# Last map of a two-layer decoder: gate products on two column tiles of the array, LoRA products on four row tiles

## Chip, cores and metric

The kernel runs on one core of a Trainium2 chip. The metric is the device time of one execution in microseconds; "us" is that throughout. Engines are named as in the profile: PE is TensorE (with PEld, its weight loads), DVE is VectorE, ACT is ScalarE, POOL is GpSimd, SP is SyncE, which issues most DMAs.

## What is computed

Two batches of 512 tokens with 1024 features pass through two decoder layers. Each layer is a cross attention and an FFN with LoRA. The change is about the very last part, the FFN of the second layer (called the last map here). Cut to what matters:

```python
x = x + _L1_xattn_ref(_layernorm(x), ctx, ctx, mask, wq, wk, wv, wo, 0)
x = x + _L1_ffn_ref(_layernorm(x), W_up, gate_w, expert_bias, lora_A, lora_B)

def _L1_ffn_ref(x, W_up, gate_w, expert_bias, lora_A, lora_B):   # E = 4 experts, R = 8
    logits = x_flat @ gate_w.T + expert_bias
    one_hot = jax.nn.one_hot(jnp.argmax(logits, axis=-1), 4)
    base_out = jnp.einsum('bth,oh->bto', x, W_up)
    z = jnp.einsum('nh,erh->ner', x_flat, lora_A)
    d = jnp.einsum('ner,ehr->neh', z, lora_B) * SCALE            # SCALE = 1
    return base_out + jnp.einsum('neh,ne->nh', d, one_hot)
```

So for every token there are 4 gate logits and 32 LoRA values (36 columns, one matrix `ga_t`), the best expert is chosen, the 8 values of that expert are kept and the other 24 are set to zero, and the 32 values are multiplied by a 32 x 1024 matrix and added to the 1024 x 1024 map. All matrix products here are in f32.

## The kernel before

**The map.** A 512 x 1024 by 1024 x 1024 product is done with seven block products in place of eight (a Winograd form of Strassen's scheme). `token_sums` makes the seven left operands from normed and transposed rows (L245, L248, L250, L253 on DVE), `right_sums` the seven right operands from four 512 x 512 quarters of the weight (L259, L262, L264, L267 on DVE). `linear` (L572) gives two chains of seven block products, one for each half of the tokens in a block, `blocks(0)` and `blocks(1)`, which `pair` interleaves for the first two products and then runs one after the other. Each block product is four accumulated matmuls of 128x128 by 128x512 on TensorE, issued by `accumulate` at L347. `seven_onto` (L304) takes them in the order 1, 2, 6, 7, 5, 4, 3 and adds them to the rows: product 1 is copied to a tile u by ACT (L315), product 6 is added to u by DVE (L317), each other product is added by DVE straight to its quarter of the rows (L320), and where u belongs too (products 5, 4 and 3), POOL adds it afterwards (L322). The row quarters are called (0,0), (1,1), (1,0) and (0,1).

**LoRA before.** `lora` in `linear` hangs one more matmul on products 2, 4, 5 and 3 of each chain: eight for a map and sixteen for the two batches. It contracts over all 128 partitions, of which 32 hold something; the rest of z and of the LoRA matrix (L1232, one load of 128 x 1024) is zero. The third operand it needs is the difference of the two token halves (`split_tokens`, L596).

**Gates before.** `gated` (L947) is a generator. For each of four groups of 128 tokens, eight matmuls take the tokens as the stationary operand (128x128) and `ga_t` (36 columns) as the moving one (L954), into one tile of type "wide". Then DVE does for each group of tokens seven small operations (L966 to L978): add the bias, take the maximum, compare, prefer the first of equals, compare again, and multiply the 32 values by the choice into a tile z, which POOL has set to zero (L976, two memsets of 128x256). Four transposes on TensorE (L988) and a DVE copy (L989) give z transposed.

**What sets the order.** TensorE's queue follows the order of the program text exactly. In the attention loop that order is written by hand for DVE, ACT and POOL as well: `attention` (L847) yields three times for each head, and `hooks` (L1194 to L1214) attach actions to a head and a phase. The last heads share their time with the beginning of the last map of batch 0: the weights are fetched at hook (61, 2), the gate products stand at (62, 1), the gate arithmetic at (62, 2), and the transposes of z with the first two block products at (63, 1). After L1236 a scheduler orders DVE, ACT, POOL and SP. There `turned_and_gated` (L1248) weaves the norms, transposes (L204) and gates of batch 1 into the map of batch 0.

**The softmax around it.** For each head POOL sums the exponentials (L811, L814, L815, L816), TensorE transposes the sums (L723), DVE reduces them (L725), and a row goes through DRAM (L732, L738); DVE adds the negative maximum to the scores (L805) and ACT takes the exponential (L808). L822 is the product with the values; the projection with wo (`projection`, L835) also goes through `seven_onto` and L347, in blocks of two matmuls.

**Buffers.** PSUM has two "wide" tiles (two banks each) and four "b" tiles (one bank each). The transposes of rows (L202) and of softmax sums (L721) use wide tiles.

Of the kernel before, what the change touches and what calls it, by code (L numbers as in the profile page):

```python
# [15 lines left out]
ALU = mybir.AluOpType  # L16
AX = mybir.AxisListType

P = 128
B, S, D = 2, 512, 1024  # L20
# [4 lines left out]
E1, R1 = 4, 8  # L25
# [6 lines left out]
NT = S // P  # L32
NC = D // P
NKT = S2 // P
HALF = 512
# [4 lines left out]
def decoder_kernel(  # L40
# [25 lines left out]
    nc = tc.nc  # L66
# [39 lines left out]
    ident = const.tile([P, P], F32, name="ident")  # L106
# [194 lines left out]
                emit(0, 1, u)  # L301
            yield

    def seven_onto(product, place, order=(1, 6, 2, 7, 5, 4, 3)):  # L304

        banks = {}
        for i in order:
            first = {2: 1, 4: 7, 3: 5}.get(i, i)
            if i == first:
                banks[i] = ps_b()  # L310
            acc = banks[first]
            product(i, acc, i == first)
            if i == 1:
                u = u2([P, HALF])
                nc.scalar.copy(u, acc)  # L315
            elif i == 6:
                nc.vector.tensor_tensor(u, u, acc, ALU.add)  # L317
            else:
                c = place(*{2: (0, 0), 7: (1, 1), 5: (1, 1), 4: (1, 0), 3: (0, 1)}[i])
                nc.vector.tensor_tensor(c, c, acc, ALU.add)  # L320
                if i != 2 and i != 7:
                    nc.gpsimd.tensor_tensor(c, c, u, ALU.add)  # L322
            yield

    def pair(a, b):
# [15 lines left out]
    def advance(stretches, n):  # L341
        for _ in range(n):
            next(stretches)
# [27 lines left out]
    def rows(b, t):  # L371
        return x[b][t // 2][:, t % 2, :]
# [158 lines left out]
    def normed(b, tile, n, ready=None):  # L531

        if n == 2:
            hs = [tile([P, 4, S]) for _ in range(2)]
            quarters = [[hs[ch][:, :, ts(th, 256)] for ch in range(2)] for th in range(2)]
        else:
            quarters = [[tile([P, 4, 256]) for _ in range(2)] for _ in range(2)]
        steps = transposed_norm(
            b,
            [[quarters[t // 2][j][:, :, ts(t % 2, P)] for t in range(NT)] for j in range(2)],  # L540
            ready,
        )
# [29 lines left out]
    def linear(b, h_ops, w_ops, tT, bl):  # L572

        def blocks(s):
            lora = {2: (0, 0), 4: (1, 0), 5: (1, 1), 3: (2, 1)}

            def product(i, acc, start):
                pairs = [
                    (h_ops[i - 1][:, c, ts(s, P)], w_ops(i, c))
                    for c in range(4)  # L580
                ]
                if i in lora:
                    th, nh = lora[i]
# [3 lines left out]
            return seven_onto(  # L587
                product,
                lambda i, j: rows(b, 2 * i + s)[:, ts(j, HALF)],
                (1, 2, 6, 7, 5, 4, 3),  # L590
            )
# [355 lines left out]
    def gated(quarters):  # L947


        zT, diff = u2([P, S]), u2([P, 256])  # L950
        gaccs = ps_wide().rearrange("p (t n) -> p t n", t=NT)
        for t in range(NT):
            for c in range(NC):
                nc.tensor.matmul(  # L954
                    gaccs[:, t, :NGA],
                    chunk(quarters, c, t),
                    ga_t[:, c, :],
                    start=(c == 0),
                    stop=(c == NC - 1),
                )  # L960
            yield
        zs = []
        for t in range(NT):
            gacc = gaccs[:, t, :]
            lg = small([P, E1])
            nc.vector.tensor_tensor(lg, gacc[:, :E1], eb_t, ALU.add)  # L966
            mx = small([P, 1])
            nc.vector.tensor_reduce(mx, lg, AX.X, ALU.max)

            nc.vector.tensor_scalar(lg, lg, mx, None, ALU.is_equal)  # L970
            nc.vector.tensor_tensor(lg, lg, prefer, ALU.mult)
            nc.vector.tensor_reduce(mx, lg, AX.X, ALU.max)
            nc.vector.tensor_scalar(lg, lg, mx, None, ALU.is_equal)
            if t % 2 == 0:
                z2 = u2([P, 2, P])
                nc.gpsimd.memset(z2, 0.0)  # L976
            z = z2[:, t % 2]
            nc.vector.tensor_tensor(  # L978
                z[:, : E1 * R1].rearrange("p (e r) -> p e r", r=R1),
                gacc[:, E1:NGA].rearrange("p (e r) -> p e r", r=R1),  # L980
                lg.unsqueeze(2).to_broadcast([P, E1, R1]),
                ALU.mult,
            )
            zs.append(z)
        yield
        tr = ps_tr()
        for t, z in enumerate(zs):
            nc.tensor.transpose(tr[:, t, :], z, ident)  # L988
        nc.vector.tensor_copy(zT, tr.rearrange("p t n -> p (t n)"))  # L989
        yield split_tokens(zT, diff)  # L990


    ctx.enter_context(tc.manual_schedule(engines={mybir.EngineType.PE}))
# [117 lines left out]
    bl_t = u8([P, D])  # L1111
# [64 lines left out]
    def turn_row(t):  # L1176
        transposed(
            last["rows"][:, t % 2, :],
            [last["hs"][t // 2][j][:, :, ts(t % 2, P)] for j in range(2)],
        )  # L1180
# [5 lines left out]
            wupT[ts(ch, 4 * P), ts(nh, HALF)].rearrange("(c p) n -> p c n", p=P),  # L1186
        )

    def begin_map():
        hs = last["hs"]  # L1190
        last["h"][:2] = hs[0]
        last["gates"] = gated(hs)

    hooks = {(42, 0): [lambda: next(stats)], (42, 1): [turn_away]}  # L1194
    for t in range(NT):
# [1 line left out]
    for i in range(2):  # L1197
        n = 44 + 4 * i
        hooks[(n, 2)] = [lambda i=i: fetch_half(i)]
        hooks[(n + 1, 1)] = [lambda i=i: scale_row(2 * i)]  # L1200
        hooks[(n + 2, 1)] = [lambda i=i: turn_row(2 * i), lambda i=i: scale_row(2 * i + 1)]
        hooks[(n + 3, 1)] = [lambda i=i: turn_row(2 * i + 1)]
    hooks[(61, 2)] = [
        lambda: fetch_weight(1, 0, 0),
        lambda: fetch_weight(2, 1, 0),
        lambda: fetch_rows(0),
        begin_map,
    ]
    hooks[(62, 1)] = [lambda: advance(last["gates"], 4)]
    hooks[(62, 2)] = [  # L1210
        lambda: next(last["gates"]),
        lambda: fetch_weight(7, 0, 1),
        lambda: fetch_weight(3, 1, 1),
    ]  # L1214
    with tc.manual_schedule(
        engines={
            mybir.EngineType.DVE,
            mybir.EngineType.Activation,
            mybir.EngineType.Pool,
        }  # L1220
    ):
        for i in range(3 * (B * NH + 2)):
            next(steps)
            n, phase = divmod(i, 3)
            for act in hooks.get((n - 2, phase), ()):
                act()
            if (n - 2, phase) == (63, 1):
                zTs = [next(last["gates"]), None]
                h_ops, parts = last["h"], last["w"]
                w_ops = lambda i, c: parts[i - 1][:, c, :]  # L1230
                bl_t = u4([P, D])
                nc.sync.dma_start(bl_t, bl1T)  # L1232
                main = linear(0, h_ops, w_ops, lambda: zTs[0], bl_t)
                advance(main, 2)

    h_ops[:] = token_sums(last["hs"], lambda: u4([P, 4, 256]))  # L1236
# [5 lines left out]
    advance(main, 5)  # L1242
    for _ in steps:
        pass
    hs, norms = normed(1, u4, 4)
    gates = gated(hs)

    def turned_and_gated():  # L1248
        next(norms)
        yield  # L1250
        next(norms)
        yield
        for _ in range(3):
            next(norms)
            next(gates)
            yield
        next(gates)
        yield
        next(gates)
        yield  # L1260
# [16 lines left out]
def rope_tables():  # L1277
# [68 lines left out]
```

## Time and profile before

| what | value |
|---|---|
| median of 3 runs | 2475.18 us (2473.69 to 2479.97) |
| profiled execution | 2474.92 us |
| its span in the trace | 2473.1 us |
| mean granted TensorE clock | 0.993 |
| TensorE idle before L347, all of the kernel | 19.1 us, most of it for the first loads |
| L954, gate products | 128 instructions of 128x36, 2273.4 to 2408 |
| L759, scores | 1024 of 128x512, 454.3 us busy |
| L773, DVE add of 128x1024 from PSUM | mean 1224 ns |
| L320, DVE add of 128x512 from PSUM | mean 680 ns |

Columns of a row are explained where it is shown. A matmul's end is modelled in the trace, so the distance between starts is a better measure of its cost than the length shown. A weight load (LDWEIGHTS) overlaps the matmul before it. A matmul in f32 shows as two pairs of weight load and matmul. The timeline merges neighbours of one kind into one line with a count.

### The profile page before, as it was taken

How to read it: one execution, taken by the hardware profiler on the slowest of the kernel's cores; microseconds unless marked ns; L12 is line 12 of the kernel's file. 1: busy time of each engine (PE TensorE's matmuls, PEld its weight loads, DVE VectorE, ACT ScalarE, POOL GpSimd, SP SyncE). 2: the span in 40 equal slices, each digit the busy share in tenths (PEclk: the TensorE clock that was granted, in tenths of full speed). 3: DMA queues.
4: the chain of work that ended last, by engine and by line, in shares of the span. 5: the costliest groups of instructions: out<-in, count | busy, mean ns of one | idle time of the engine just before them, and what ended most of it. 6: DMA issues, size and time to landing. Idle time of an engine off the chain costs nothing.

```text
span 2473.1 us, 19694 instructions
## 1 busy us (share of the span) xinstructions
PE 2432.6 (98%) x6856; PEld 1218.4 (49%) x6856; DVE 1835.2 (74%) x2020; ACT 528.1 (21%) x615; POOL 1028.8 (42%) x552
## 2 busy tenths in 40 slices
PE   8999999999999999999999999999999999999998
PEld 3477458654444444444444444444444444445453
DVE  4949674346886547898888888888888888886552
ACT  1211221001122222222222222222222222222100
POOL 0000010111000002686767767776767676767421
PEclk9999999999999999999999999999999999999999
DMA  5437142013895221344323432443334333323301
GB/s 181 179 120 255 69 146 97 22 68 111 296 333 187 74 98 41 106 128 115 103 76 90 115 95 81 128 149 89 105 110 129 79 94 108 112 72 103 128 26 43
DMA packets 148819, 288.02 MB, mean 116 GB/s; under 512 B 29360, under 2 KB 47296, under 8 KB 146416
## 3 DMA queue, kind: packets, MB, share of 16 engines
q1 hardware_dynamic: 107888, 244.35, 29.4%
q10 hardware_dynamic: 40400, 41.70, 6.9%
q8 instruction: 55, 0.90, 0.2%
q0 software_dynamic: 432, 0.71, 0.1%
q14 instruction: 44, 0.36, 0.1%
HBM read 223.54 MB, written 63.18 MB: 116 GB/s over the span
## 4 chain that ended last, share of the span: by engine, by line
PE 79%; DVE 8%; POOL 3%; issue 2%; DMA 2%; ACT 1%; SPq 0%; ACTq 0%; POOLq 0%; DVEq 0%
PE b L347 45%; PE wide L759 15%; PE b L822 14%; DVE u L805 2%; PE wide L723 2%; PE wide L460 1%; PE wide L204 1%; POOL u L815 1%; POOL u L814 1%; DVE u L783 1%; DMA u<-in_wo_dram 1%; DVE u L785 1%; PE wide L954 1%; DVE small L725 1%; DMA row<-small 1%
## 5 line engine op out<-in xcount | busy, mean ns | idle before, releaser
L347 PE MATMUL b<-u,u 128*128 128x512 f32 (+1 forms) x3648 | 1407.8, 544 | 19.1 <-DMA u<-in_ctxT_in_dram 7.8
L347 PEld LDWEIGHTS b<-u,u 128*128 128x128 f32 x3648 | 693.6, 191 | 698.7 <-issue 619.2
L822 PE MATMUL b<-u,u 128*128 128x512 f32 x1024 | 462.3, 595 | 0.0
L759 PE MATMUL wide<-u,u 128*128 128x512 f32 x1024 | 454.3, 595 | 7.2 <-DVE u L773 6.3
L773 DVE TENSOR_TENSOR u<-wide,u 128x1024 f32<-128x1024 f32 x256 | 312.9, 1224 | 133.1 <-PE wide L759 132.9
L808 ACT ACTIVATE u<-u 128x2048 f32<-128x2048 f32 x128 | 244.6, 1911 | 653.8 <-DVE u L805 619.9
L759 PEld LDWEIGHTS wide<-u,u 128*128 128x128 f32 x1024 | 193.9, 190 | 256.0 <-issue 176.7
L805 DVE TENSOR_TENSOR u<-u,b 128x2048 f32<-128x2048 f32 x128 | 290.2, 2268 | 0.0
L811 POOL TENSOR_TENSOR u<-u 128x1024 f32<-128x1024 f32 x64 | 151.4, 2366 | 319.8 <-ACT u L808 319.8
L822 PEld LDWEIGHTS b<-u,u 128*128 128x128 f32 x1024 | 187.3, 193 | 185.6 <-issue 185.6
L322 POOL TENSOR_TENSOR u<-u,u 128x512 f32<-128x512 f32 x120 | 188.7, 1592 | 197.5 <-DVE u L320 177.9
L320 DVE TENSOR_TENSOR u<-u,b 128x512 f32<-128x512 f32 x200 | 135.9, 680 | 135.4 <-PE b L347 135.4
L222 POOL TENSOR_TENSOR u<-u,sin_t 128x512 f32<-128x512 f32 x8 | 11.6, 1455 | 387.8 <-ACT u L217 387.8
L814 POOL TENSOR_TENSOR u<-u,u 128x1024 f32<-128x1024 f32 x64 | 150.8, 2356 | 35.6 <-ACT u L808 35.2
L815 POOL TENSOR_TENSOR u<-u,u 128x1024 f32<-128x1024 f32 x64 | 151.6, 2369 | 5.0
L833 POOL TENSOR_TENSOR u<-u,u 128x512 f32<-128x512 f32 x64 | 117.7, 1839 | 21.8 <-DMA u<-row 21.8
L216 ACT ACTIVATE u<-u 64x512 f32<-64x512 f32 x72 | 45.2, 628 | 356.1 <-DVE u L293 177.9
L603 POOL TENSOR_TENSOR u<-u,u 128x1024 f32<-128x1024 f32 x8 | 20.2, 2532 | 231.5 <-DVE u L168 228.9
L723 PEld LDWEIGHTS wide<-ident,u 128*128 128x128 f32 x512 | 80.1, 204 | 64.5 <-issue 54.3
L781 DVE TENSOR_TENSOR u<-u 128x1024 f32<-128x1024 f32 x64 | 110.4, 1725 | 0.0
L783 DVE TENSOR_TENSOR u<-u,u 128x1024 f32<-128x1024 f32 x64 | 106.1, 1658 | 0.2
L816 POOL TENSOR_TENSOR u<-u 128x512 f32<-128x512 f32 x64 | 101.4, 1584 | 5.0
(127 smaller groups left out, 1624.8 us busy)
## 6 DMA issues: line engine op xcount, KB each, us to landing
u<-row ACTq DMA_DIRECT2D x128, 256.0 KB, 3.7
u<-wo SPq DMA_DIRECT2D x64, 512.0 KB, 4.2
u<-in_wo_dram SPq DMA_DIRECT2D x48, 512.0 KB, 4.5
u<-in_wq_dram SPq DMA_DIRECT2D x32, 512.0 KB, 4.2
q<-u SPq DMA_DIRECT2D x64, 256.0 KB, 2.6
u<-in_wo_dram SPq DMA_DIRECT2D x16, 1024.0 KB, 8.1
wo<-u SPq DMA_DIRECT2D x32, 512.0 KB, 4.4
u<-q SPq DMA_DIRECT2D x64, 256.0 KB, 4.2
```

Of the source, the lines that this page charges most:

```text
L320: nc.vector.tensor_tensor(c, c, acc, ALU.add)
L322: nc.gpsimd.tensor_tensor(c, c, u, ALU.add)
L347: nc.tensor.matmul(acc, lhsT, rhs, start=start and k == 0, stop=k == len(pairs) - 1, skip_group_check=True,)
L759: nc.tensor.matmul(sc[:, ts(n, HALF)], self.kT[:, ts(2 * j + n, P)], self.qT, start=True, stop=True,)
L773: nc.vector.tensor_tensor(self.e[j // 2][:, js, :], sc.rearrange("p (k q) -> p k q", k=2), mask[j], ALU.add)
L783: nc.vector.tensor_tensor(m, m, e[1][:, 0:2, :], ALU.max)
L805: nc.vector.tensor_tensor(e, e, self.nmf.unsqueeze(1).to_broadcast([P, 4, S]), ALU.add)
L808: nc.scalar.activation(e, e, AF.Exp)
L811: nc.gpsimd.tensor_tensor(d, e[:, 0:2, :], e[:, 2:4, :], ALU.add)
L814: nc.gpsimd.tensor_tensor(d, d, e[:, 0:2, :], ALU.add)
L815: nc.gpsimd.tensor_tensor(d, d, e[:, 2:4, :], ALU.add)
L822: nc.tensor.matmul(self.acc, self.v[:, k, :], self.e[j][:, k % 4, :], start=(k == 0), stop=(k == NKT - 1),)
```

## The change

Gates: `ga_t` becomes the stationary operand (36 columns) and 256 tokens the moving one, so that 16 matmuls do what 32 did. Even chunks of the contraction go to partitions 0 to 35 of a bank and odd ones to 64 to 99; that places them on the two 64-column tiles of the array. ACT copies both halves to a tile that POOL has set to zero one phase earlier, TensorE transposes that tile (four), and DVE adds the two halves and does the gate arithmetic for all four groups of tokens at once. z is written four times side by side, so that its transpose holds it on partitions 0, 32, 64 and 96.

LoRA: the products leave `linear`, and `split_tokens` is no longer called here. `add_lora` makes two parts of four matmuls, each with 32 rows of contraction on a row tile of its own and into a bank of its own (two wide tiles), and DVE adds them to the rows. The matrix is loaded four times, to 32 partitions each. The parts stand between products of the map.

Rows: with `u_first`, which every `linear` now uses (both FFNs), POOL adds u to the three quarters as soon as product 6 is in, ahead of DVE's adds of products 7, 5, 4 and 3. Row tile 1 of batch 1, the last to be complete, is stored in two halves.

In the queues, the zeros go to hook (61, 1), the gate products and their arithmetic both to (62, 1). On SP the load of weight quarter 7 goes ahead of three wo loads and that of quarter 3 ahead of two.

```diff
-    def seven_onto(product, place, order=(1, 6, 2, 7, 5, 4, 3)):
+    def seven_onto(product, place, order=(1, 6, 2, 7, 5, 4, 3), u_first=False):
...
             elif i == 6:
                 nc.vector.tensor_tensor(u, u, acc, ALU.add)
+                if u_first:
+                    for k in (5, 4, 3):
+                        add(place(*places[k]), u)
             else:
-                c = place(*{2: (0, 0), 7: (1, 1), 5: (1, 1), 4: (1, 0), 3: (0, 1)}[i])
+                c = place(*places[i])
                 nc.vector.tensor_tensor(c, c, acc, ALU.add)
-                if i != 2 and i != 7:
-                    nc.gpsimd.tensor_tensor(c, c, u, ALU.add)
+                if i != 2 and i != 7 and not u_first:
+                    add(c, u)
...
-            lora = {2: (0, 0), 4: (1, 0), 5: (1, 1), 3: (2, 1)}
+            lora = {} if tT is None else {2: (0, 0), 4: (1, 0), 5: (1, 1), 3: (2, 1)}
...
     def gated(quarters):
-        zT, diff = u2([P, S]), u2([P, 256])
-        gaccs = ps_wide().rearrange("p (t n) -> p t n", t=NT)
-        for t in range(NT):
+        sums = u2([P, S])
+        nc.gpsimd.memset(sums, 0.0)
+        yield
+        parts = [slice(64 * i, 64 * i + NGA) for i in range(2)]
+        for th in range(2):
+            acc = ps_b()
             for c in range(NC):
                 nc.tensor.matmul(
-                    gaccs[:, t, :NGA],
-                    chunk(quarters, c, t),
+                    acc[parts[c % 2], 0:256],
                     ga_t[:, c, :],
-                    start=(c == 0),
-                    stop=(c == NC - 1),
+                    quarters[th][c // 4][:, c % 4, :],
+                    start=(c < 2),
+                    stop=(c >= NC - 2),
                 )
-            yield
+            for part in parts:
+                nc.scalar.copy(sums[part, ts(th, 256)], acc[part, 0:256])
+            yield
...
+        for t in range(NT):
+            nc.tensor.transpose(tr[:, t, :], sums[:, ts(t, P)], ident)
+        nc.vector.tensor_copy(both, tr[:, :, parts[0]])
+        nc.vector.tensor_tensor(both, both, tr[:, :, parts[1]], ALU.add)
...
+        for k in range(4):
             nc.vector.tensor_tensor(
-                z[:, : E1 * R1].rearrange("p (e r) -> p e r", r=R1),
...
+                z[:, :, ts(k, E1 * R1)].rearrange("p t (e r) -> p t e r", r=R1),
...
+    def add_lora(b, zT, bl):
+        K = E1 * R1
+        for i in range(2):
+            accs = [ps_wide() for _ in range(2)]
+            for k in range(4):
+                j, nh = k // 2, k % 2
+                nc.tensor.matmul(
+                    accs[j][:, ts(nh, HALF)],
+                    zT[ts(k, K), ts(2 * i + j, P)],
+                    bl[ts(k, K), ts(nh, HALF)],
+                    start=True,
+                    stop=True,
+                )
+            for j in range(2):
+                xs = rows(b, 2 * i + j)
+                nc.vector.tensor_tensor(xs, xs, accs[j], ALU.add)
+            yield
...
+    hooks[(61, 1)] = [begin_gates]
...
-    hooks[(62, 1)] = [lambda: advance(last["gates"], 4)]
+    hooks[(62, 1)] = [lambda: advance(last["gates"], 3)]
     hooks[(62, 2)] = [
-        lambda: next(last["gates"]),
...
-                nc.sync.dma_start(bl_t, bl1T)
-                main = linear(0, h_ops, w_ops, lambda: zTs[0], bl_t)
+                for k in range(4):
+                    nc.sync.dma_start(bl_t[ts(k, E1 * R1), :], bl1T[: E1 * R1, :])
+                main = linear(0, h_ops, w_ops, None, None)
...
     def turned_and_gated():
+        next(lora)
         next(norms)
         yield
...
+        next(gates)
         next(norms)
         yield
-        for _ in range(3):
-            next(norms)
-            next(gates)
-            yield
+        next(norms)
+        yield
         next(gates)
+        next(lora)
         yield
...
-    main = linear(1, token_sums(hs, lambda: u4([P, 4, 256])), w_ops, lambda: zTs[1], bl_t)
+    main = linear(1, token_sums(hs, lambda: u4([P, 4, 256])), w_ops, None, None)
     advance(main, 2)
-    zTs[1] = next(gates)
+    zT = next(gates)
+    lora = add_lora(1, zT, bl_t)
+    for _ in range(2):
+        advance(main, 2)
+        next(lora)
...
-    for t in range(NT):
+    for t in (0, 2, 3):
         nc.sync.dma_start(out[1, ts(t, P), :], rows(1, t))
+    for i in range(2):
+        nc.sync.dma_start(out[1, ts(1, P), ts(i, HALF)], rows(1, 1)[:, ts(i, HALF)])
```

More of the change, by code (lines that the diff above doesn't have):

```diff
@@ L302, in seven, with add @@
             yield
-    def seven_onto(product, place, order=(1, 6, 2, 7, 5, 4, 3)):
+    def seven_onto(product, place, order=(1, 6, 2, 7, 5, 4, 3), u_first=False):
         banks = {}
+        places = {2: (0, 0), 7: (1, 1), 5: (1, 1), 4: (1, 0), 3: (0, 1)}
+        def add(c, what):
+            nc.gpsimd.tensor_tensor(c, c, what, ALU.add)
         for i in order:
@@ L590, in blocks @@
                 (1, 2, 6, 7, 5, 4, 3),
+                True,
             )
@@ L957, in gated @@
                     ga_t[:, c, :],
-                    start=(c == 0),
-                    stop=(c == NC - 1),
-                )
+                    quarters[th][c // 4][:, c % 4, :],
+                    start=(c < 2),
+                    stop=(c >= NC - 2),
+                )
+            for part in parts:
+                nc.scalar.copy(sums[part, ts(th, 256)], acc[part, 0:256])
             yield
-        zs = []
+        zT = u2([P, S])
+        z = u2([P, NT, P])
+        tr, both = ps_tr(), u2([P, NT, NGA])
@@ L963, in gated @@
         for t in range(NT):
[L964 to L977, printed above, removed]
+            nc.tensor.transpose(tr[:, t, :], sums[:, ts(t, P)], ident)
+        nc.vector.tensor_copy(both, tr[:, :, parts[0]])
+        nc.vector.tensor_tensor(both, both, tr[:, :, parts[1]], ALU.add)
+        lg = small([P, NT, E1])
+        by_expert = lambda t: t.unsqueeze(1).to_broadcast([P, NT, E1])
+        nc.vector.tensor_tensor(lg, both[:, :, :E1], by_expert(eb_t), ALU.add)
@@ L978, in gated @@
+        mx = small([P, NT])
+        by_token = mx.unsqueeze(2).to_broadcast([P, NT, E1])
+        nc.vector.tensor_reduce(mx, lg, AX.X, ALU.max)
+        nc.vector.tensor_tensor(lg, lg, by_token, ALU.is_equal)
+        nc.vector.tensor_tensor(lg, lg, by_expert(prefer), ALU.mult)
+        nc.vector.tensor_reduce(mx, lg, AX.X, ALU.max)
+        nc.vector.tensor_tensor(lg, lg, by_token, ALU.is_equal)
+        for k in range(4):
             nc.vector.tensor_tensor(
-                z[:, : E1 * R1].rearrange("p (e r) -> p e r", r=R1),
@@ L980, in gated @@
-                gacc[:, E1:NGA].rearrange("p (e r) -> p e r", r=R1),
-                lg.unsqueeze(2).to_broadcast([P, E1, R1]),
+                z[:, :, ts(k, E1 * R1)].rearrange("p t (e r) -> p t e r", r=R1),
+                both[:, :, E1:].rearrange("p t (e r) -> p t e r", r=R1),
+                lg.unsqueeze(3).to_broadcast([P, NT, E1, R1]),
                 ALU.mult,
             )
-            zs.append(z)
         yield
         tr = ps_tr()
-        for t, z in enumerate(zs):
-            nc.tensor.transpose(tr[:, t, :], z, ident)
+        for t in range(NT):
+            nc.tensor.transpose(tr[:, t, :], z[:, t, :], ident)
@@ L989, in gated @@
         nc.vector.tensor_copy(zT, tr.rearrange("p t n -> p (t n)"))
-        yield split_tokens(zT, diff)
+        yield zT
+    def add_lora(b, zT, bl):
[15 more added lines that the diff above has]
+            yield
@@ L1187, in fetch_weight, with begin_gates @@
         )
[L1189 to L1192, printed above, removed]
+    def begin_gates():
+        last["h"][:2] = last["hs"][0]
+        last["gates"] = gated(last["hs"])
+        next(last["gates"])
     hooks = {(42, 0): [lambda: next(stats)], (42, 1): [turn_away]}
@@ L1206, in decoder_kernel @@
         lambda: fetch_rows(0),
-        begin_map,
     ]
-    hooks[(62, 1)] = [lambda: advance(last["gates"], 4)]
+    hooks[(62, 1)] = [lambda: advance(last["gates"], 3)]
     hooks[(62, 2)] = [
-        lambda: next(last["gates"]),
         lambda: fetch_weight(7, 0, 1),
@@ L1227, in decoder_kernel @@
             if (n - 2, phase) == (63, 1):
-                zTs = [next(last["gates"]), None]
+                zT = next(last["gates"])
                 h_ops, parts = last["h"], last["w"]
@@ L1244, in decoder_kernel @@
         pass
+    lora = add_lora(0, zT, bl_t)
     hs, norms = normed(1, u4, 4)
     gates = gated(hs)
+    next(gates)
     def turned_and_gated():
+        next(lora)
+        next(norms)
+        yield
+        for _ in range(2):
+            next(norms)
+            yield
+        next(gates)
         next(norms)
@@ L1267, in decoder_kernel @@
         nc.sync.dma_start(out[0, ts(t, P), :], rows(0, t))
-    main = linear(1, token_sums(hs, lambda: u4([P, 4, 256])), w_ops, lambda: zTs[1], bl_t)
+    main = linear(1, token_sums(hs, lambda: u4([P, 4, 256])), w_ops, None, None)
     advance(main, 2)
-    zTs[1] = next(gates)
+    zT = next(gates)
+    lora = add_lora(1, zT, bl_t)
+    for _ in range(2):
+        advance(main, 2)
+        next(lora)
     for _ in main:
         pass
-    for t in range(NT):
+    for t in (0, 2, 3):
         nc.sync.dma_start(out[1, ts(t, P), :], rows(1, t))
+    for i in range(2):
+        nc.sync.dma_start(out[1, ts(1, P), ts(i, HALF)], rows(1, 1)[:, ts(i, HALF)])
 def rope_tables():
```

## The prediction

> **What bounds the kernel now.** I read the page first: the share of each engine, then the chain that ended last.
>
> ```profile
> span 2473.1 us, 19694 instructions
> PE 2432.6 (98%) x6856; PEld 1218.4 (49%) x6856; DVE 1835.2 (74%) x2020; ACT 528.1 (21%) x615; POOL 1028.8 (42%) x552
> PE 79%; DVE 8%; POOL 3%; issue 2%; DMA 2%; ACT 1%; SPq 0%; ACTq 0%; POOLq 0%; DVEq 0%
> ```
>
> TensorE is the bound nearly everywhere: what leaves its queue in the last map is gained, unless something else is then late. The change touches only the end, so next I read TensorE's timeline there (start, length to the modelled end, line, form, count; in brackets the idle time and its releaser).
>
> ```profile
> 2266.96 7.03 PE L347 MATMUL b<-u,u 128*128 128x512 f32 x16
> 2273.83 9.84 PE L954 MATMUL wide<-ga_t,u 128*128 128x36 f32 x64
> 2283.47 1.10 PE L723 MATMUL wide<-ident,u 128*128 128x128 f32 x4
> 2284.36 9.00 PE L822 MATMUL b<-u,u 128*128 128x512 f32 x16
> 2293.19 5.31 PE L347 MATMUL b<-u,u 128*128 128x512 f32 x12
> ...
> 2303.81 0.48 PE L988 MATMUL b<-ident,u 128*128 128x128 f32 x1 [0.93 <-DVE u L978]
> 2304.08 9.37 PE L347 MATMUL b<-u,u 128*128 128x512 f32 x16
> ```
>
> A product in f32 appears as two instructions: 4 x 8 gate products are x64. The x16 groups of one form are 6.87 us apart at 2266.96 and 9.21 at 2304.08. The windows (length, then busy time of PE, weight load, DVE, ACT, POOL, then PEclk, the granted clock) tell why:
>
> ```profile
> 2274.00:2277.00 3.00, 3.00 (x30) 3.00 (x29) 0.69 (x1) 0.59 (x1) 2.92 (x3) 1.00 0.56 87
> 2280.00:2284.00 4.00, 4.00 (x21) 4.00 (x21) 0.00 (x0) 0.00 (x0) 1.50 (x2) 0.50 0.00 0
> 2284.00:2288.00 4.00, 4.00 (x8) 1.94 (x7) 3.36 (x4) 0.29 (x1) 0.00 (x0) 0.50 0.02 1
> 2300.00:2305.00 5.00, 1.99 (x5) 0.99 (x6) 4.39 (x22) 0.00 (x0) 0.00 (x0) 0.70 1.03 398
> ```
>
> The 36-column gate products are paced by weight loads (PEld full) and the clock falls to half during them; it falls again where TensorE waits for the gate arithmetic. The last view is DVE, which shows what that wait was for, and the end of the chain:
>
> ```profile
> 2292.51 2.01 DVE L973 TENSOR_SCALAR small<-small,small 128x4 f32<-128x4 f32 x1
> 2298.55 0.19 DVE L978 TENSOR_TENSOR u<-wide,small 128x32 f32<-128x32 f32 x1 [4.03 <-POOL u L976]
> ```
>
> ```profile
> 2462.64 0.70 DVE u L320
> 2463.34 0.07 issue
> 2463.40 1.26 POOL u L322
> ```
>
> The zeros (L976) stand in POOL's queue behind the softmax sums; DVE waited 4.03 us for them, then did four tokens' gates one after another. At the very end a POOL add follows the DVE add.
>
> **Stretch A, first gates, 2273.83 to 2320.63: 46.80 us of TensorE.** Its parts, start to start: gates 9.64, transposes L723 0.89, L822 8.83, L347 5.31, waits with z transposes 5.58, first map products 9.21, L723 0.47, L822 6.87.
>
> New gates: 16 products, 32 instructions of 256 columns. The nearest row is the 128x256 group of the first FFN, x32 in 6.91 us: serial, that is no less than 64 x 0.107 = 6.84 us, the old gates at full clock (1.71 per 16). All gain in gates alone must come from overlap. No tiled product is in this trace, so the bounds are 6.91 (none) and 3.45 (perfect). The two instructions of a product stand together on one column tile, so the second can overlap only the first of the next product on the other tile: 16+1 steps of 0.216 = 3.67 us. I take that. Then TensorE has nothing but the transposes of the sums, which wait for two ACT copies of 36x256; ACT's 128x512 copies are 0.58, so I estimate 0.37 each and 0.9 with handover; ACT stands idle from 2274.70 to 2277.62 before, so no exponential is in the way. New: 3.67 + 0.90 + 0.47 + L723 0.47 + L822 6.87 + L347 5.15 + z transposes 0.47 + map 6.87 + L723 0.47 + L822 6.87 = 32.2. Gain 14.6.
>
> Is something else late? POOL's memset now lands in its idle stretch 2259.06 to 2267.61 (two of 128x256 took 0.56) and holds up nothing. DVE's batched gate arithmetic is 13 instructions: two of 144 elements (0.33 each; a 256-element one is 0.42), six small (0.2 with gaps), four of 128 elements (0.31): 3.1 us, against 1.46 for each of four tokens. It starts at 2279.0 and is done at 2282.1; the reduction L725 and exponent adds L805 queue behind it and start at 2283.0, before it was 2285.42. From there to the last softmax sum on POOL took 12.84 us (2298.26), so 2295.9; TensorE asks for that sum at 2298.7. Cover 2.8 us; if DVE slips more, TensorE waits for the rest. The z transposes are asked for at 2291.4: 9 us cover.
>
> On SP, the fetch of weight 7 now stands ahead of three wo loads, that of weight 3 ahead of two. They wait for the last heads' L822 (issued 2293.51 and 2317.43 before), which come earlier themselves; the wo loads behind are used some 30 us later. Four loads of the LoRA matrix replace one (0.46 each to issue), needed 60 us later. Nothing.
>
> **Stretch B, to the wait on L267 (2372.27).** Three LoRA products go (two instructions of 0.43 each): 2.6 us. The 0.84 us wait stays, since DVE's L267 stands behind adds of the same TensorE products.
>
> **Stretch C, to TensorE's end at 2466.89.** Out: 13 LoRA products, 11.2 us, and gates 6.87. In: gates 2 x 9 steps = 3.9, transposes of sums 0.44, four LoRA parts of four products on four row tiles. Unoverlapped a part is x8 of 128x512, 3.44 us. By the same pairing it is 5 steps of 8, 2.15, four of them 8.6. [...] I take 2.15. Gain 11.2 + 6.87 - 3.9 - 0.44 - 8.6 = 5.1.
>
> [...]
>
> The LoRA sums are eight DVE adds of 128x1024 from PSUM, 1.22 each by L773: 9.8 us. DVE is busy 6.83 of 2380 to 2400 and 3.45 of 2420 to 2440, so they fit. Where they bind is the wide buffer: part one holds both, and the next row's transposes (L204) need one back. After the part TensorE has one product, 3.44; DVE needs L320 0.69, L168 0.80 (these beside the part) and the add 1.22. Cover about 1 us; missed, it costs one or two once.
>
> **The u adds.** In both FFNs POOL adds u first, three adds from i=6 on. DVE's add for i=7 now waits on the first, 1.26 us (2.5 beside a long DVE instruction); the i=7 products last 3.44. No cost; in the first FFN one bias add (L603, 2.35) moves behind them, used 40 us later. Without cover it would be 1 to 2 us a block. At the end the POOL add is gone, 1.33, and the last store is half as large: 512 KB to the output landed in 2.6 us, the 256 KB stores of kT, v and q in 2.0 to 2.6, so 0 to 0.6, I take 0.3. Gain 1.6.
>
> **Sum.** 14.6 + 2.6 + 5.1 - 1.5 + 1.6 = 22.4. The profiled execution took 2474.92 us with a span of 2473.1; the median of the runs is 0.26 above it. 2475.18 - 22.4 = 2452.8.
>
> **Rivals.** (1) Tiles do not overlap in f32: gates +3.2 and +3.0, LoRA +5.2: 2464.2. For it: no row here shows overlap. It is still faster, because the zeros, the wait and the half clock go anyway. [...] (3) The column-tiled gates, with 36 of 128 columns in use, let the clock fall as before. Before, it was half for some 10.6 us after 2278; new, that lies over L822, 5.3 lost: 2458.1. Against it: the old products streamed 36 columns in the time of 128, the new ones stream all the time. (4) Slower: the same fall at every tiled stretch of the last map, where now full-width products keep the clock at 1.00. There are seven of these (first gates, two second gates, four LoRA parts), 5.3 each: 37 us, 2490. It decides from five on (22.4 / 5.3 = 4.2). (5) The order of DVE or SP binds (wide buffer, sums late): some 4 to 12 us lost, 2457 to 2465.
>
> **Numbers.** My forecast 0.5, (1) 0.22, (2) 0.1, (3) 0.06, (4) 0.04, (5) 0.08. The range runs from (2) with no drains, 2447, to (1) with all drains, 2466. Faster by over 0.3% (7.4 us, about what a measurement can tell from no change) is every case but (4), and the worst of (1), (3) and (5) together: 0.89; within 0.05; slower 0.06.
>
> **What would show it.** Right: the new gate group lasts under 4 us with a clock of 1.00, one short TensorE wait on ACT copies, no idle time on the zeros or z; L822 in 6.87; LoRA groups near 2.2; the chain ends in a DVE add. Wrong: gate groups of 6.9 and LoRA parts of 3.4 (rival 1), PEclk below 1 after tiled products (3, 4), TensorE idle on a LoRA add at L204 or on L725's chain (5).

## The result, and the profile after

The change makes the kernel faster: 2450.33 us, median of 5 runs (2448.16 to 2455.72), against 2475.18 for before, also 5 runs (2473.69 to 2479.97). The ratio is 0.9901, with a 95% interval of 0.9891 to 0.9912. The profiled execution of after took 2450.07 us. These are the page's lines that answer to those shown of before:

```profile
span 2448.3 us, 19583 instructions
PE 2412.5 (99%) x6792; PEld 1195.8 (49%) x6800; DVE 1841.1 (75%) x1994; ACT 530.8 (22%) x623; POOL 1031.3 (42%) x550
PE 60%; DVE 6%; POOL 2%; issue 1%; DMA 1%; ACT 1%; ACTq 0%; SPq 0%; DVEq 0%; POOLq 0%
```

TensorE lost 20.1 us of busy time (2432.6 to 2412.5), most of the 24.8 us by which the span became shorter. L347 of before is L355 here, L822 is L831, L320 is L328, L315 is L320, L954 is L967; around the softmax, L732 is L741, L738 is L747, L805 is L814, L808 is L817 and L830 is L839. TensorE's timeline in stretch A, from the first gate product on:

```profile
2274.92 3.89 PE L967 MATMUL b<-u,ga_t 128*36 128x256 f32 x32
2278.73 0.44 PE L981 MATMUL b<-ident,u 128*128 128x128 f32 x2
2279.65 0.44 PE L981 MATMUL b<-ident,u 128*128 128x128 f32 x2 [0.48 <-ACT u L975]
2279.92 0.64 PE L732 MATMUL wide<-ident,u 128*128 128x128 f32 x4
2280.40 7.03 PE L831 MATMUL b<-u,u 128*128 128x512 f32 x16
2287.27 3.60 PE L355 MATMUL b<-u,u 128*128 128x512 f32 x8
2293.35 1.99 PE L355 MATMUL b<-u,u 128*128 128x512 f32 x4 [2.48 <-ACT u L320]
2295.17 0.60 PE L1005 MATMUL b<-ident,u 128*128 128x128 f32 x4
```

The gates take 3.81 us from start to start, against 9.64, and L831 6.87 (2280.40 to 2287.27). No wait on z or the zeros is left. But there is a wait that was not there before: 2.48 us in the middle of L355. The end of the same timeline, stretch C:

```profile
2358.88 3.70 PE L355 MATMUL b<-u,u 128*128 128x512 f32 x8 [0.84 <-DVE u L267]
2362.51 1.14 PE L1016 MATMUL wide<-u,u 32*128 32x512 f32 x8
2363.59 3.70 PE L355 MATMUL b<-u,u 128*128 128x512 f32 x8
...
2375.84 1.92 PE L967 MATMUL b<-u,ga_t 128*36 128x256 f32 x16
2377.69 1.09 PE L204 MATMUL wide<-ident,u 128*128 128x128 f32 x8
```

A LoRA part of four products lasts 1.07 to 1.08 us (2362.51 to 2363.59), the gates of half a batch 1.85. The clock (last but two of the columns) stays at full speed in all of the last map, here in the first gates and in stretch C:

```profile
2274.90:2278.70 3.80, 3.76 (x33) 1.74 (x32) 0.69 (x1) 1.32 (x3) 3.72 (x3) 1.00 0.38 66
2358.90:2444.50 85.60, 85.60 (x272) 38.48 (x272) 38.88 (x63) 5.75 (x13) 13.62 (x11) 1.00 0.12 47
```

The chain of work ends as foreseen in DVE's add, with no POOL behind it:

```profile
2444.63 0.04 issue
2444.67 0.69 DVE u L328
```

**Where the time went.** By starts in the two timelines: stretch A 46.80 to 34.89, a gain of 11.9; stretch B 51.64 to 49.07, 2.57; stretch C from the wait on L267 to TensorE's end, 94.62 to 85.68, 8.94; from TensorE's end to the span's, 6.2 to 3.7, 2.5. Together 25.9. The first gates started 1.09 us later than before (2274.92 against 2273.83), which leaves 24.8. That is within the spread of this start: with the same program text up to there it came anywhere from 2271.0 (e5) to 2274.92, so the experiments are compared from the first gate product to TensorE's end (called G below): 193.06 before, 169.65 after.

**What the new wait is.** ACT's timeline at that place:

```profile
2284.92 0.33 ACTq L741 DMA_DIRECT2D row<-small  x1
2287.10 1.91 ACT L817 ACTIVATE u<-u 128x2048 f32<-128x2048 f32 x1 [7.02 <-DVE u L814]
2289.90 0.34 ACTq L747 DMA_DIRECT2D u<-row  x1
2290.29 1.91 ACT L817 ACTIVATE u<-u 128x2048 f32<-128x2048 f32 x1 [1.28 <-DMA row<-small]
2292.22 0.58 ACT L839 COPY u<-b 128x512 f32<-128x512 f32 x1
2292.70 0.59 ACT L320 COPY u<-b 128x512 f32<-128x512 f32 x1
```

The row of softmax sums goes to DRAM (L741) and back (L747), and both transfers are issued by ACT. L747 waits until the row has landed, and behind it in ACT's queue stand the second exponential, the copy L839 and the copy L320 of product 1, which frees the PSUM buffer that TensorE wants. In before, ACT was ahead, and its copies waited for TensorE:

```profile
2285.54 0.33 ACTq L732 DMA_DIRECT2D row<-small  x1
2287.71 1.91 ACT L808 ACTIVATE u<-u 128x2048 f32<-128x2048 f32 x1 [9.50 <-DVE u L805]
2288.02 0.33 ACTq L738 DMA_DIRECT2D u<-row  x1
2289.91 1.91 ACT L808 ACTIVATE u<-u 128x2048 f32<-128x2048 f32 x1 [0.29 <-DVE u L805]
2293.39 0.58 ACT L830 COPY u<-b 128x512 f32<-128x512 f32 x1 [1.57 <-PE b L822]
2295.16 0.58 ACT L315 COPY u<-b 128x512 f32<-128x512 f32 x1 [1.19 <-PE b L347]
```

| us from the first gate product to | before | after | sooner by |
|---|---|---|---|
| TensorE's L347 / L355, after the product with the values | 19.36 | 12.35 | 7.0 |
| DVE's adds L805, L814 | 11.59 | 9.88 | 1.7 |
| first exponential | 13.88 | 12.18 | 1.7 |
| second exponential | 16.08 | 15.37 | 0.7 |
| copy of product 1 | 21.33 | 17.78 | 3.6 |

So most of the wait is that the exponentials, which stand behind DVE's adds, come so little sooner. The row adds to it: it took 4.98 us from issue to issue, against 2.48 before. DVE's second add ended at 2289.25 and the second exponential began at 2290.29, so the row can have cost about 1.0 of the 2.48 us at most. In e5 the same difference is 0.2 (2285.81 to 2286.04), and the wait is 2.37 all the same.

DMA's share of the row's window is 0.93 in after and 0.03 in before. The load of x (L402) is issued at 2284.07 in after, just ahead of the row; in before (L394) it was issued at 2289.99, behind it. A faster TensorE moved that load as well. This crowding was not tried by itself. Other runs fit it in part: share 0.39 and 2.80 us in e8, where the x load is issued 0.27 us behind the row, 0.75 and 4.64 in e7.

### The profile page after: what moved, and what is told of

It reads as the page before. It is cut to its first block, busy times and chain, and to the rows that moved or that the text cites. A ratio compares the mean times of both kernels' runs of the same rounds, so it can differ in the third digit from the quotient of the medians.

```text
span 2448.3 us, 19583 instructions
## 1 busy us (share of the span) xinstructions
PE 2412.5 (99%) x6792; PEld 1195.8 (49%) x6800; DVE 1841.1 (75%) x1994; ACT 530.8 (22%) x623; POOL 1031.3 (42%) x550
## 4 chain that ended last, share of the span: by engine, by line
PE 60%; DVE 6%; POOL 2%; issue 1%; DMA 1%; ACT 1%; ACTq 0%; SPq 0%; DVEq 0%; POOLq 0%
PE b L355 26%; PE wide L768 16%; PE b L831 15%; PE wide L732 2%; DVE u L814 2%; DMA u<-in_wo_dram 1%; DVE u L782 1%; POOL u L823 0%; POOL u L824 0%; DVE small L734 0%; DVE u L792 0%; DVE u L794 0%; ACT u L817 0%; POOL u L825 0%; DVE u L328 0%
## 5 line engine op out<-in xcount | busy, mean ns | idle before, releaser
L355 PE MATMUL b<-u,u 128*128 128x512 f32 (+1 forms) x3616 | 1394.2, 542 | 21.3 <-DMA u<-in_ctxT_in_dram 7.6
L355 PEld LDWEIGHTS b<-u,u 128*128 128x128 f32 x3616 | 684.6, 191 | 695.9 <-issue 612.8
L831 PE MATMUL b<-u,u 128*128 128x512 f32 x1024 | 460.3, 592 | 0.0
L817 ACT ACTIVATE u<-u 128x2048 f32<-128x2048 f32 x128 | 244.7, 1912 | 655.8 <-DVE u L814 593.9
L814 DVE TENSOR_TENSOR u<-u,b 128x2048 f32<-128x2048 f32 x128 | 290.2, 2268 | 0.0
L831 PEld LDWEIGHTS b<-u,u 128*128 128x128 f32 x1024 | 186.2, 192 | 184.6 <-issue 184.6
L328 DVE TENSOR_TENSOR u<-u,b 128x512 f32<-128x512 f32 x200 | 135.8, 680 | 126.0 <-PE b L355 125.9
L790 DVE TENSOR_TENSOR u<-u 128x1024 f32<-128x1024 f32 x64 | 115.8, 1810 | 0.0
L732 PEld LDWEIGHTS wide<-ident,u 128*128 128x128 f32 x512 | 79.6, 203 | 63.9 <-issue 55.0
L825 POOL TENSOR_TENSOR u<-u 128x512 f32<-128x512 f32 x64 | 101.0, 1578 | 5.0
```

The source lines that it names most:

```text
L355: nc.tensor.matmul(acc, lhsT, rhs, start=start and k == 0, stop=k == len(pairs) - 1, skip_group_check=True,)
L732: nc.tensor.transpose(tr[:, t, :], src[:, t, :], ident)
L814: nc.vector.tensor_tensor(e, e, self.nmf.unsqueeze(1).to_broadcast([P, 4, S]), ALU.add)
L817: nc.scalar.activation(e, e, AF.Exp)
L831: nc.tensor.matmul(self.acc, self.v[:, k, :], self.e[j][:, k % 4, :], start=(k == 0), stop=(k == NKT - 1),)
```

## The experiments

My theory after the result: (1) a product on a tile waits only for its own tile; (2) the 2.48 us are ACT's queue, and no engine's throughput; (3) zeros and rows are worth little by themselves. The rival to (1) was the pairing of the prediction, in which a product's second instruction keeps later products from starting.

**e1: which tile each LoRA product is on.** The four parts of the change get four different choices of row tiles:

```diff
+                r = ((0, 1, 2, 3), (0, 1, 0, 1), (0, 0, 1, 1), (0, 0, 0, 0))[2 * b + i][k]
-                    zT[ts(k, K), ts(2 * i + j, P)],
-                    bl[ts(k, K), ts(nh, HALF)],
+                    zT[ts(r, K), ts(2 * i + j, P)],
+                    bl[ts(r, K), ts(nh, HALF)],
```

> The changed kernel, but only the first LoRA part of batch 0 uses four row tiles in the order 0,1,2,3. The second part uses two tiles in the order 0,1,0,1, the first part of batch 1 two tiles in the order 0,0,1,1, the last part tile 0 alone; the values are the same, since z and the matrix lie on every tile. Theory (a product waits only for its own row tile, wherever it stands in the text): 1.07, then about 1.9 and 1.9 (four steps of 0.43 and a drain), then 3.5 us. Rival (products start in the order of the text, the pairing of the prediction): 1.07 stays unexplained, 0,1,0,1 takes 5 steps, 2.15 to 2.3, and 0,0,1,1 takes 7 steps, 3.0. Rival (the gain is not from the tiles but from K=32 alone): 1.07 in all four.

Measured: 2456.75 us in one run. TensorE's timeline, the last three parts, each with the group behind it:

```profile
2390.74 1.99 PE L1017 MATMUL wide<-u,u 32*128 32x512 f32 x8
2392.65 3.70 PE L355 MATMUL b<-u,u 128*128 128x512 f32 x8
...
2410.90 1.99 PE L1017 MATMUL wide<-u,u 32*128 32x512 f32 x8
2412.82 7.13 PE L355 MATMUL b<-u,u 128*128 128x512 f32 x16
...
2419.88 3.70 PE L1017 MATMUL wide<-u,u 32*128 32x512 f32 x8
2423.51 27.73 PE L355 MATMUL b<-u,u 128*128 128x512 f32 x64
```

Four tiles take 1.07 us (2364.94 to 2366.01), two tiles in turn 1.91, two tiles one after the other (0,0,1,1) 1.92, one tile 3.63. What the expectation calls a drain is the 0.21 us by which the 1.07 is longer than two steps of 0.43. The times go with the products on the fullest tile (one 1.07, two 1.91 and 1.92, four 3.63), and the two orders on two tiles differ by 0.01. Pairing falls: it wants 0,0,1,1 to be dearer than 0,1,0,1. Four tiles are 3.63 / 1.07 = 3.4 times as fast as one, so both instructions of an f32 product overlap; in the trace of after all four first instructions start within 0.02 us, at 2362.515 to 2362.535. The other rival, that 32 rows of contraction are the gain, wants 1.07 everywhere and falls too. G is 176.44, 6.8 above after's: 4.2 are the three altered parts, and the rest lies at the wait on ACT (3.22 us here) and in slower groups behind it (2.98 us for the x4 group of L355, 1.82 in after; 0.85 for the z transposes, 0.44 in after).

**e2: order and tile of the gate products.** In batch 1, first half: even chunks, then odd ones. Second half: all on one column tile.

```diff
+            one = (b, th) == (1, 1)
+            order = (0, 2, 4, 6, 1, 3, 5, 7) if (b, th) == (1, 0) else range(NC)
+            for c in order:
-                    acc[parts[c % 2], 0:256],
+                    acc[parts[0 if one else c % 2], 0:256],
```

> The changed kernel, with the gate products of batch 1 altered: its first half takes the even chunks first and then the odd ones (so the column tiles no longer alternate in the text), its second half puts all eight chunks on the first column tile (one ACT copy fewer, the other half of the sums stays zero). Theory (a product waits only for its own tile): 1.85 for the first, 3.45 for the second, against 1.85 for both in the changed kernel. Rival (order matters, TensorE looks ahead by only a few products): 3.3 for the first. Rival (no column overlap, the products are short for another reason): 1.85 for both.

Measured: 2453.6 us in one run, and in TensorE's timeline:

```profile
2376.73 2.81 PE L969 MATMUL b<-u,ga_t 128*36 128x256 f32 x16
2379.48 1.09 PE L204 MATMUL wide<-ident,u 128*128 128x128 f32 x8
...
2388.24 3.64 PE L969 MATMUL b<-u,ga_t 128*36 128x256 f32 x16
2391.82 1.14 PE L1018 MATMUL wide<-u,u 32*128 32x512 f32 x8
```

Evens then odds take 2.75 us, one tile 3.58, in turn 1.85. The 2.75 is neither theory (1.85) nor rival (3.3): order does matter in this run of four on one tile, but less than the rival said. An estimate from these times: at 3.58 / 8 = 0.45 us a product, 1.85 is 4.1 products one behind the other and 2.75 is 6.1, as if the four odd products began with the third even one. Then one waiting product, the fourth even one, would have been passed, and no more: a theory for e8.

**e8: look-ahead, and clock without overlap.** Batch 0: all gate products on one column tile. Batch 1: other orders of the chunks.

```diff
+            one = b == 0
+            if b == 1:
+                order = ((0, 2, 1, 3, 4, 6, 5, 7), (0, 2, 4, 1, 3, 5, 6, 7))[th]
+            for c in order:
-                    acc[parts[c % 2], 0:256],
+                    acc[parts[0 if one else c % 2], 0:256],
```

> The change, with the gate products in other places and another order; no value differs. Batch 0: all 16 gate products on one column tile. Batch 1: the even chunks still on one tile and the odd ones on the other, but the text's order of chunks is 0,2,1,3,4,6,5,7 in the first half and 0,2,4,1,3,5,6,7 in the second. Look-ahead theory (a product that waits for its own tile lets one product behind it go ahead): first half 1.85 us, as in the alternating order; second half about 2.2; evens then odds took 2.75 before. Rival, strict order (whatever stands behind a waiting product waits too): 2.2 and 2.6. Clock: if it is the 36-column streams that brought it down before, and not the lack of overlap, batch 0's block takes about 7.1 us (2 x 3.58) in place of 3.6 at a granted clock of 1.00; if the overlap of two tiles is what keeps it up, the clock falls below 0.9 in it and the block takes over 7.5, and the 128x512 group after it more than 6.9. The whole: 2453 to 2455, up to 3.5 more where the wait on the row's copy doesn't hide part of it.

Measured: 2450.57 us in one run. TensorE's timeline, with the first gates and both halves of batch 1:

```profile
2274.34 7.10 PE L971 MATMUL b<-u,ga_t 128*36 128x256 f32 x32
2281.37 0.96 PE L985 MATMUL b<-ident,u 128*128 128x128 f32 x4
...
2293.33 1.98 PE L355 MATMUL b<-u,u 128*128 128x512 f32 x4 [0.22 <-ACT u L320]
2295.15 0.60 PE L1009 MATMUL b<-ident,u 128*128 128x128 f32 x4
...
2375.81 1.95 PE L971 MATMUL b<-u,ga_t 128*36 128x256 f32 x16
2377.69 1.09 PE L204 MATMUL wide<-ident,u 128*128 128x128 f32 x8
...
2386.46 2.38 PE L971 MATMUL b<-u,ga_t 128*36 128x256 f32 x16
2388.77 1.14 PE L1020 MATMUL wide<-u,u 32*128 32x512 f32 x8
```

The halves of batch 1 take 1.88 and 2.31 us. Look-ahead by one product was to give 1.85 and about 2.2, strict order 2.2 and 2.6. The measured times lie 0.03 and 0.1 from the first and 0.3 from the second, so theory (1) needs a limit in the gates, and of the two the look-ahead is the one that fits. It fits e1, too: in 0,0,1,1 only one product waits ahead of the first on the other tile (1.92 against 1.91 in turn). That is read from the lengths of groups; how TensorE does it was not shown.

The first gates without overlap take 7.03 us. The granted clock is 1.00 in them, so overlap is not needed for it here. In before, with 64 instructions of the old form in a row (36 streamed columns for each weight load), it was 0.68 from 2277 to 2280 and 0.50 from 2280 to 2288. The old form's groups of 16 in batch 1 took 1.71 us each, at a clock of 1.00.

The surprise is the line of L1005 (L1009 here). From the first gate product to it, after takes 20.25 us and e8 20.81. Overlap in the first gates saves 3.2 us (7.03 - 3.81) and brings only 0.56, since the new wait on ACT's copy is 2.48 with it and 0.22 without, and the 0.48 us wait on the copies of the sums is there only with it. The waits take most of it back. By an estimate, about 1.0 of that is the crowded row, which e8 does not have: ACT is idle for 0.29 us ahead of its second exponential there, and for 1.28 in after. The rest of e8 fits: G is 170.68, 1.04 above after's, and 0.56 + 0.46 (2.31 against 1.85 in the last half) is 1.02.

**e3: the zeros alone.** The kernel before, with all zeros set at hook (61, 1) and nothing else:

```diff
+        z2s = [u2([P, 2, P]) for _ in range(2)]
+        for z2 in z2s:
+            nc.gpsimd.memset(z2, 0.0)
+        yield
-            if t % 2 == 0:
-                z2 = u2([P, 2, P])
-                nc.gpsimd.memset(z2, 0.0)
-            z = z2[:, t % 2]
+            z = z2s[t // 2][:, t % 2]
```

> The kernel before, with nothing changed but the zeros of z: POOL sets them at hook (61, 1), as in the changed kernel. Theory A (the 4.03 us wait on the zeros is what TensorE lost): the waits around the z transposes shrink from 5.58 to about 1.5 us and the second fall of the clock (2.3 us) goes, 2469. Theory B (DVE's gate operations are late anyway, since its TENSOR_SCALAR on 4 elements takes about 2 us while POOL sums): only some 2 us, 2473, and the clock falls as before.

Measured: 2473.13 us against 2474.22, ratio 0.9992 (0.9984 to 1.0001); G 190.40, which is 2.7 less. The waits around the z transposes fell from 5.58 to 4.19 us and the map group behind them from 9.21 to 8.11. DVE shows why the 4.03 us of waiting on the zeros were worth so little:

```profile
2290.96 2.37 POOL L811 TENSOR_TENSOR u<-u 128x1024 f32<-128x1024 f32 x1 [8.54 <-ACT u L808]
2291.24 0.16 DVE L972 TENSOR_REDUCE small<-small 128x1 f32<-128x4 f32 x1
2291.43 1.92 DVE L974 TENSOR_SCALAR small<-small,small 128x4 f32<-128x4 f32 x1
...
2293.77 2.02 DVE L977 TENSOR_SCALAR small<-small,small 128x4 f32<-128x4 f32 x1
...
2302.67 0.23 DVE L977 TENSOR_SCALAR small<-small,small 128x4 f32<-128x4 f32 x1
```

A TENSOR_SCALAR on 128x4 elements takes up to 2.02 us beside POOL's adds (2290.96 to 2300.76), and 0.23 afterwards. It ends when POOL's add ends: L974 at 2293.35, L811 at 2293.33. All five in that stretch end 0.02 to 0.04 us behind a POOL add, while the reduction beside the same add takes 0.16. With the zeros at hand, DVE does its work earlier, but in the stretch in which it is slow. So the zeros alone bring at most 2.7 of the 11.9 us of stretch A. The rest is left to the gates, since the rows bring nothing there (e4) and LoRA has no part in it (e5); how it divides between the shorter products, the clock and the batched arithmetic ahead of POOL's sums was not tried.

**e4: the rows alone.** The kernel before, with `u_first` and the split last store, as in the change's diff:

```diff
+                if u_first:
+                    for k in (5, 4, 3):
+                        add(place(*places[k]), u)
...
+    for i in range(2):
+        nc.sync.dma_start(out[1, ts(1, P), ts(i, HALF)], rows(1, 1)[:, ts(i, HALF)])
```

> The kernel before, with only the rows part of the change: u added by POOL first, the last row tile stored in two halves. Theory: from the last matmul to the end 3.7 us in place of 6.2, so 2.5 faster, 2472.7, and nothing else moves. Rival (POOL adds that DVE now waits for delay the map or the first FFN): less than 2.5, down to a loss, with TensorE idle before products 4 or 3 of a chain.

Measured: 2473.1 us, ratio 0.9994 (0.9986 to 1.0003). The chain ends, as in after, in DVE's add L328, at 2467.01, and TensorE's work at 2466.91. G is 193.06, as before: u first costs TensorE nothing. From TensorE's end to the span's it is 4.1 us, against 6.2: 2.1 gained, in the medians 1.1 with an interval that includes none. The part is real in the trace, and too small for the medians.

**e5: the change without its LoRA part.** LoRA as before in `linear`, everything else as in after:

```diff
-        yield zT
+        yield split_tokens(zT, u2([P, 256]))
...
-                main = linear(0, h_ops, w_ops, None, None)
+                main = linear(0, h_ops, w_ops, lambda: zTs[0], bl_t)
```

> The changed kernel with LoRA as before: sixteen full-width products inside the map, the matrix loaded once with its zero rows, the difference of the token halves. Gates, zeros and rows as in the change. Theory (the LoRA tiles are worth what the trace of the changed kernel shows: 16 products of 0.86 less four parts of 1.07 and their drains): 8 to 9 us slower than the changed kernel, 2459. Rival (the LoRA products filled time that is now a wait, or the DVE adds cost elsewhere): under 5 us slower, 2455 or less.

Measured: 2461.69 us (2456.78 to 2462.44), ratio 0.9944 (0.9925 to 0.9962); G 179.84, so 10.5 more than e7's. Of that, 1.7 is no LoRA work. In e5 the same wait (2.37 us) is followed by a lower clock, which after (1.00 from 2293.30 to 2302.50) and e7 (1.00 from 2292.90 to 2302) did not show:

```profile
2289.10:2292.00 2.90, 2.90 (x5) 1.24 (x6) 0.69 (x1) 0.00 (x0) 2.82 (x2) 0.66 1.06 405
```

The clock was 0.91 in the 8 us after that. The three groups behind the wait take 1.7 us longer here than at full clock (the first of them 2.70 in place of 1.82). Why the clock fell behind 2.37 us of waiting here, and not behind 2.48 in after and 2.39 in e7, was not shown. The LoRA part is worth the rest, 8.9: 2.6 in stretch B and 6.3 in stretch C. That is one trace, of the fastest execution of e5; by the medians e5 is 12.0 us slower than e7, more than the 8 to 9 expected, and one trace does not settle where the rest lies.

**e6: the wait taken away.** After, with the copy of product 1 done by DVE in the one place where it stood behind the row:

```diff
+                copy=nc.vector.tensor_copy if late and s else None,
...
-                nc.scalar.copy(u, acc)
+                (copy or nc.scalar.copy)(u, acc)
```

> The changed kernel, and in the second chain of the last projection but one, product 1 is copied to u by DVE in place of ACT. Theory (the new idle time of 2.48 us before the third L355 group of that chain is product 1's copy behind ACT's DMA wait and its second exponential): the wait goes, z is asked for 2.65 us sooner, and the end comes 2.6 us earlier, 2447.7. Rival (with that wait gone the softmax sum of the last head is late: POOL ends it at 2299.3 in the changed kernel, TensorE would ask for it at 2299.8): a new wait of 0 to 1 us before L732, so 1.6 to 2.6 us gained.

Measured: 2446.82 us (2445.15 to 2449.64), ratio to before 0.9892 (0.9872 to 0.9912). TensorE's timeline:

```profile
2284.61 5.31 PE L355 MATMUL b<-u,u 128*128 128x512 f32 x12
2289.76 0.60 PE L1009 MATMUL b<-ident,u 128*128 128x128 f32 x4
...
2297.43 0.75 PE L732 MATMUL wide<-ident,u 128*128 128x128 f32 x4 [0.20 <-POOL u L825]
```

The wait is gone: L355 is one x12 group of 5.15 us from start to start, as the prediction had it. What is late next is the last sum on POOL (L825), by 0.20 us, as the rival in the expectation had it. G is 167.15, 2.2 below e7's. This is the best version by median and trace; its interval overlaps e7's, so the medians by themselves don't prove the 2 us.

**e7: the change again**, unaltered, on the chip of e5 and e6.

> The changed kernel once more, on the same chip as the two others: 2450 us, 24 to 25 us faster than before.

Measured: 2449.68 us (2448.14 to 2451.94), ratio 0.9900 (0.9884 to 0.9917); G 169.31; the wait 2.39 us. So the wait belongs to the kernel and not to one execution: it is 2.37 to 3.22 in after, e1, e2, e5 and e7.

## Why the prediction was right, and where two errors met

The time was 2450.33 where 2452.8 was predicted. The sum of gains was to be 22.4 and is 24.8 by the two spans. Its parts were less good than that, and that their errors met is luck:

| step | predicted | measured |
|---|---|---|
| stretch A | 14.6 | 11.9 |
| stretch B | 2.6 | 2.57 |
| stretch C, the 1.5 taken off | 3.6 | 8.94 |
| end | 1.6 | 2.5 |
| start of the first gates | 0 | -1.09 |

- **Stretch A, gates.** The size was right: 3.67 predicted for the products; 3.59 in e7, and 3.81 in after, where the second half started 0.2 us late, behind ACT's copy L839. The pairing behind it was not: by it the second product starts one step of 0.216 behind the first, and in after the two start at 2274.916 and 2274.922. With two tiles that is one step in 17 and doesn't show. One wait of 0.48 us on ACT's copies, as said. L831 and the x16 group of the map at 6.87, as said.
- **Stretch A, "Is something else late?"** This step failed. It asked that of DVE, POOL and SP, and of ACT only whether it is free when the gates are copied. What the earlier loads would fall on was not asked either, and everything that ACT owes after the gates was left out: its second exponential comes only 0.7 us sooner, and product 1's copy, which stands behind it, 3.6, while TensorE comes 7.0 sooner. L355 takes 7.90 us from its first start to the z transposes in place of 5.15. e6 takes that cause away and finds the 5.15. Part of it could be read from the prediction's own figures: exponent adds from 2283.0 (4.45 us for two), an exponential (1.91) and two copies (about 0.6 each) end at about 2290.5, and TensorE would want the buffer at about 2289.6, an estimated wait of 0.9.
- **The cover of POOL's last sum.** 2.8 us was taken; in e6, where TensorE comes on time, the sum is 0.20 late. The gate arithmetic (twelve instructions, not thirteen; the 3.1 counts twelve) took 3.95 us in after, since two of them, L986 and L991, ended with a POOL add (0.50 and 0.98). From L814 to the last sum it was 15.03 in e6, not 12.84. In after the wait on ACT hid this.
- **z transposes.** The "9 us cover" was right: nothing waited for them.
- **Stretch B.** Right, with the 0.84 us wait where it was.
- **Stretch C, LoRA.** That the row tiles overlap was right; the pairing was wrong, and here it shows: 2.15 a part was taken from it, 1.07 was measured, so 4 x 1.08 = 4.3 us more gain. The pairing was an assumption of the author's: no row of before shows it, and e1 speaks against it. The gates of batch 1 took 1.85 a half where 1.94 was taken.
- **The 1.5, the range's drains.** No run shows this term of the sum. What the runs show in its place: the groups of L355 beside a LoRA part take longer (x16: 6.97 ahead of one, 7.06 between two, 6.87 elsewhere), some 0.1 on each side. But before's groups beside its gates had such a loss too (x8: 3.52, and 3.43 elsewhere). Added up, the 168 instructions of L355 in stretch C take 73.26 us; L347 took 83.87 there, less 26 LoRA instructions at 0.429, so 72.71. The net price of these groups is 0.55.
- **The end.** POOL's add is gone, 1.33 as said. (The prediction's lines of it belong to the last product but one; the last pair, at 2466.93 and 2467.70, has the same lengths.) From the last add's end to the span's end it was 4.1 before and is 2.9 after: with the split store it is 1.2 less, not 0.3, and 0.8 less in e4 (3.3).
- **The u adds.** No cost, as said (e4).
- **Rivals.** (1) falls in every row. The range's lower end, 2447, and the chance of 0.1 that goes with it ask for more overlap of the row tiles than the pairing allows: no row of before shows such an overlap, and what the runs show is 1.07 us a part on four tiles and 3.63 on one (e1). (3) and (4) fall: the clock is 1.00 in the first gates and in all of stretch C, and in e8 even without overlap. (5) named the kind of thing that came, an order that binds, but not the engine.

Stretch C adds up: 3.6 + 4.3 for the parts + 0.2 for the gates + 1.0, since 0.55 stands in place of the 1.5, is 9.1, and 8.94 was measured.

So the total came out near because +5.3 in stretch C and +0.9 at the end met -2.7 in stretch A and -1.1 ahead of it.

## What to carry to other kernels

When an engine's stretch becomes 7 us shorter, look at every queue that serves it in the order of the text, as ACT's did here (2.48 us of waiting on a copy), including DMA issues that wait for a landing, and ask for each when its next item is due relative to the new start. Ask also which loads start sooner, and what they then fall on. Overlap that ends in front of such a queue brings little: on ACT's wait, 3.2 us of faster gates became 0.56. Products on separate row or column tiles overlapped nearly fully in f32 here (3.4 times on four row tiles, 1.9 on two row or two column tiles), so count the tile with most products, and in the text take the tiles in turn (1.85 us for half the gates, against 1.88 to 2.75 in the other orders).

## What was not expected of the hardware

- The order of the text counts on two column tiles, in steps: 1.88 us for 0,2,1,3,4,6,5,7 (e8), 2.31 for 0,2,4,1,3,5,6,7 (e8) and 2.75 for 0,2,4,6,1,3,5,7 (e2), against 1.85 in turn.
- The wait on ACT's copy was followed by slower groups in some runs and not in others, at about the same length. The x4 group of L355 behind it took 1.82 us in after (wait 2.48) and e7 (2.39), both at a granted clock of 1.00; it took 2.26 in e2 (2.53), 2.70 in e5 (2.37, clock 0.66) and 2.98 in e1 (3.22). In before the clock fell without idle time ahead of it: TensorE was busy for all of the 3.42 us from 2274.65 to 2278.07, with old gate products, and the clock was 0.50 for the 10.24 us behind them. What decides was not shown.
- Some small DVE operations took longer beside POOL's adds: TENSOR_SCALAR on 128x4 elements up to 2.02 us (e3, and 0.23 afterwards), and a TENSOR_TENSOR on 128x16 with both operands in SBUF 0.98 (L991 in after, and 0.17 in e8, where no POOL add ran). Each ended 0.02 to 0.04 us behind the POOL add that it met. A reduction (0.16, L972 in e3) and a TENSOR_TENSOR that reads a PSUM tile (0.15, L970 in e3) were as short beside POOL's first add there as without one.
- The stretch ahead of the first gates, the same in all versions of after, ended at 2271.0 to 2274.9; what moves it was not looked for.
